# A four-layer graph network on one core: the last experts add into the output by DMA, and the seams between stages are re-ordered

## The chip, the cores and the metric

The kernel runs on one core of a Trainium2 chip, as one program with one launch. The metric is the device time of an execution in microseconds (us). The core's engines run side by side, each in its own order: TensorE (PE in the profile, PEld for its weight loads), VectorE (DVE), ScalarE (ACT), GpSimd (POOL) and SyncE (SP). Sixteen DMA engines move data; ACT, SP and POOL issue the DMAs, each into a queue of its own, and only POOL issues those that take their rows from a list of indices. PSUM, TensorE's result memory, has eight banks.

## The reference

The input is a graph of 1250 nodes with 512 float32 features and 21,250 edges (20,000 and a self-loop each). Four layers follow, and each has the form

```python
xn = _layernorm(x)
x = x + gnn(xn, edges) + mix(xn)
x = x + ffn(_layernorm(x))
```

The parts that differ by layer:

- Layer 0: gnn is GATv2, three times over. Per edge `m = leaky_relu(xl[src] + xr[dst] + ef)`, a softmax over each node's incoming edges of `m @ att`, and the sum of `xl[src]` by these weights; then a layer norm and relu. ffn is a mixture of 8 experts with Sinkhorn routing.
- Layer 1: gnn is two GAT layers with 4 heads, mix an attention without a sequence product (softmax of k over the nodes). ffn has two shared experts and 8 routed ones.
- Layer 2: gnn is an EGC convolution (a normalised sum over neighbours of `x @ W_bases`, combined by weights of `x @ W_comb`), mix a linear attention. ffn has a convolution as router, shared convolutions over the nodes, 10 experts of which each node takes 2, and a layer norm at the end.
- Layer 3: gnn is a GCN, `segment_sum(h[row] * norm, col)`, mix a linear attention. ffn is a mixture of 32 experts, of which each node takes the 2 likeliest; each expert has room for 98 rows (1.25 x 2500 / 32, rounded up):

```python
dest = jnp.where(keep, a * C + pos, N * C)
buf = jnp.zeros((N * C, D)).at[dest].set(x_flat[token], mode='drop').reshape(N, C, D)
o = relu(buf @ W1 + b1) @ W2 + b2
y_flat = segment_sum(o[dest] * w[:, None], token)      # w: the gate, 0 where not kept
y_flat = where(sum of a token's w <= 1e-12, x_flat, y_flat)
```

## The kernel before

**Tiling.** The nodes are 10 tiles of 128 rows (NP = 1280). `x` stays on chip; weights come in through `weight()` (line 138), a DMA of 1 MB on SP's queue into one of four buffers. Most of the code is handed to a planner, which orders each engine's instructions by when it reckons they can run and places the buffers; in a `manual_schedule` block the named engine keeps the order written. `psum(mm, tp, more)` (line 106) divides PSUM's banks for a stage; the next division can be used only when the last reader of the old one is through. `gather` (line 231) and `scatter` (line 239) are POOL's indexed DMAs.

**Stages by time in the trace of before.** 0 to 320: layer 0's attention and the preparation of the edges. To 1590: GATv2, three calls of `gat_layer`. To 1848: `layer0_ffn`. To 2070: `global_attention` (layer 1's mix). To 2830: `gat_dense`. To 3057: `layer1_ffn`. To 3345: `layer2_attn`. To 3728: `layer2_ffn`. To 4125: `layer3_attn`. To 4488: `layer3_ffn`.

**GATv2** (`gat_layer`, line 1200 on). The edges are in 47 groups (FG) of four tiles of 128 (GE); one step of the main loop (line 1460) is one tile. `load(g)` gathers rows of the table xl for a group (four gathers on POOL, 9 buffers). `fields(g)` (line 1255) loads, on SP, the packed node numbers `nb` (4 buffers) and the edge fields into the lower rows of `oh` (3 buffers); `onehot(g)` (line 1272) expands `nb` on ACT. `right(i)` (1282) is TensorE's product of one-hot rows with the tables for xr and the edge term; DVE adds it to xl (1299) and takes the logit (1302); `spread` turns weights into one-hots and the product at line 1353 sums them by node. `finish` ends a block of nodes; `across` (line 1405) turns its rows and queues, tile by tile, the products that make the next layer's tables (`gat_tables`: four products for xl, its write `xl<-tlo` at line 1184, four for xr, its write). The next layer's gathers start when tile 9's xl is written.

**Layer 0's ffn to layer 1.** At the end of `layer0_ffn` (lines 1783 to 1792) each tile gathers its two expert rows, adds them, and is normalised and turned. `global_attention` loads wk at its start and wv later. Beside both, `count` steps build a table of edge counts. `clear` zeroes the expert buffers.

**Layer 2.** `layer1_ffn` and `layer2_attn` share one PSUM division (4, 4, 0), `layer2_ffn` has its own (3, 3, 2). In `layer2_attn` (from line 2590) each tile's neighbour sum `y` takes an mm bank, with attention steps (`go()`) between. In `layer2_ffn` the shared convolutions are a generator of steps (`shared()`), and `experts(..., beside)` runs some of them ahead of the experts and between: `beside(-1)` ten, then two at each point i, none at i = 7 to 9.

**Layer 3's attention.** `tail_steps` (line 2375) finishes layer 2's ffn tile by tile inside layer 3: its `need(t)`, with POOL's order written out, fetches a tile's two expert rows (line 231), adds them, scales and normalises them (`z*ga` on POOL, line 2897), adds them to x (185), and turns the tile. The GCN's product with `L3_gnn_W` follows each tile; the linear attention (`linear_attention_steps`, line 734), whose first weights are loaded at the start, runs beside the GCN's gathers later.

**Layer 3's ffn** (line 3036). The router gives each node's two experts, its places (`putI`) and gates (`w0`). Weights are loaded 11 ahead (line 3051). 20 scatters put rows into `routed_in` (CAP = 98 rows per expert), tiles of x get the b2 term (lines 3149 to 3153, 185) and rows without an expert (1811). Per expert: `xe` in by ACT's queue (3160), four transposes (3164), a copy `xT`, 16 products with w1 (179), relu on ACT (3169), 4 products with w2 (3173), a copy `o` (134), a write to `routed_out`. After all 32, 20 gathers and adds (231, 1811), and ten writes `out<-x` (3188).

## Time and profile before

| what | value |
|---|---|
| median of 3 runs | 4464.39 us (4461.85 to 4471.24) |
| profiled execution, its own time | 4489.82 us |
| its span | 4487.9 us, mean granted clock 0.937 |
| TensorE busy | 3922.2 us, 87% of the span |
| VectorE busy | 2689.5 us, 60% |
| ScalarE busy | 1622.8 us, 36% |
| GpSimd busy | 1351.0 us, 30% |
| DMA | 647.58 MB, mean 144 GB/s |

The profiled execution took 1.9 us more than its span, and 25.4 us more than the median. How to read its rows: a row of the timeline or of the chain gives start, duration, engine, line, operation, output<-input, and in brackets the idle time of that engine before it with what ended it. SPq, ACTq and POOLq are the issues of DMAs. A row of waits gives the waiting engine and line, what it waited for, the total in us, how often, and the longest. A row of a window gives from:to, length, busy time with count for PE, PEld, DVE, ACT, POOL, then TensorE's granted clock, the busy share of the DMA engines and GB/s. By stage, TensorE is busy 1113 of 1270 us in GATv2, 324 of 397 in layer 3's attention, 290 of 363 in its ffn.

### The profile page before, as it was taken

What the parts mean: (1) busy time and instruction counts of PE and PEld (TensorE: products, weight loads), DVE (VectorE), ACT (ScalarE), POOL (GpSimd) and SP (SyncE); (2) the same over time, 40 slices, a digit from 0 to 9 for tenths busy, and PEclk for the clock granted to TensorE, in tenths of its full rate; (3) what the DMA queues carried; (4) which work ended last, traced back from release to release, by engine and by line L of the source; (5) the groups of instructions that cost most, each with busy time, mean ns of one, the idle gap of its engine ahead of it and who ended that gap; (6) DMA issues with size and microseconds to landing.
All of it is one profiled execution on the core that took longest, in us unless ns stands there. A gap on an engine that the chain in (4) does not pass through costs nothing. (4 is left out here: it accounts for less than half of the span.)

```text
span 4487.9 us, 49486 instructions
## 1 busy us (share of the span) xinstructions
PE 3922.2 (87%) x15466; PEld 2415.7 (54%) x15466; DVE 2689.5 (60%) x6338; ACT 1622.8 (36%) x2976; POOL 1351.0 (30%) x1308
## 2 busy tenths in 40 slices
PE   5987998899788867799999999997979896898796
PEld 3434554455354434444788877563546562455474
DVE  5357895888398865523896767314584225687301
ACT  2222442344133375110464446223451232554121
POOL 2017773776466501102000000103131013675102
PEclk9988999999899988899999999999989998997798
DMA  6437664666466423402421110383002653666695
GB/s 220 159 84 211 198 199 150 198 197 193 141 179 189 145 74 108 119 17 64 146 70 42 46 35 29 143 298 128 12 27 83 233 189 119 182 200 199 225 339 181
DMA packets 283001, 647.58 MB, mean 144 GB/s; under 512 B 61673, under 2 KB 108905, under 8 KB 267322
## 3 DMA queue, kind: packets, MB, share of 16 engines
q1 hardware_dynamic: 169290, 357.13, 24.1%
q0 software_dynamic: 73088, 234.75, 18.3%
q10 hardware_dynamic: 40352, 52.44, 3.4%
q8 instruction: 127, 2.08, 0.2%
q14 instruction: 144, 1.18, 0.1%
HBM read 528.87 MB, written 120.65 MB: 145 GB/s over the span
## 5 line engine op out<-in xcount | busy, mean ns | idle before, releaser
L231 POOL DMA_INDIRECT xl<-xl,srcI x564 | 616.8, 1094 | 290.2 <-issue 137.8
L1353 PE MATMUL more<-xl,wT 128*128 128x512 f32 x1128 | 579.7, 601 | 14.5 <-ACT wT L1343 14.0
L1286 PE MATMUL mm<-hl,oh 121*128 121x512 f32 x564 | 419.1, 743 | 73.8 <-DVE s L1299 37.8
L1302 DVE SCALAR_TENSOR_TENSOR junk<-s,att 128x512 f32<-128x512 f32 x534 | 417.9, 783 | 6.8
L1299 DVE TENSOR_TENSOR s<-xl,mm 128x512 f32<-128x512 f32 x534 | 357.8, 679 | 104.0 <-PE mm L1287 48.4
L2129 PE MATMUL more<-hh,e 128*128 128x259 f32 x1600 | 383.7, 385 | 11.7 <-ACT o L2072 8.6
L2129 PEld LDWEIGHTS more<-hh,e 128*128 128x128 f32 x1600 | 295.1, 191 | 75.8 <-issue 17.8
L171 PE MATMUL mm<-w,xnT 128*128 128x512 f32 x640 | 307.8, 620 | 16.6 <-ACT xnT L2388 12.1
L231 POOL DMA_INDIRECT hs<-gcn_h,srcI x188 | 214.6, 1142 | 93.6 <-issue 30.8
L1353 PEld LDWEIGHTS more<-xl,wT 128*128 128x128 f32 x1128 | 196.1, 192 | 74.8 <-issue 27.9
L1287 PE MATMUL mm<-hl,oh 121*128 121x512 f32 x564 | 236.4, 419 | 0.0
L1286 PEld LDWEIGHTS mm<-hl,oh 121*128 121x128 f32 x564 | 111.0, 197 | 215.5 <-issue 117.1
L231 POOL DMA_INDIRECT g<-routed_out,getI x60 | 67.6, 1126 | 488.5 <-DMA routed_out<-o 416.4
L2049 ACT ACTIVATE e<-r,hh 128x512 f32<-128x512 f32 (+1 forms) x240 | 154.2, 646 | 130.7 <-PE more L2129 119.5
L171 PEld LDWEIGHTS mm<-w,xnT 128*128 128x128 f32 x640 | 123.4, 198 | 144.0 <-issue 124.6
L3011 PE MATMUL more<-hl,oh 128*128 128x512 f32 x376 | 161.5, 534 | 30.9 <-DVE oh L2975 10.9
L1273 ACT ACTIVATE oh<-nb 112x512 fp32r<-112x512 bf16 x141 | 88.7, 630 | 273.6 <-DMA nb<-nbt 162.3
L2052 ACT ACTIVATE e<-r,a 128x512 f32<-128x512 f32 (+1 forms) x240 | 152.3, 646 | 71.1 <-DVE e L2054 57.8
L711 PE MATMUL more<-ohs,ohb 128*128 128x512 bf16 x564 | 137.5, 383 | 42.8 <-ACT ohs L695 18.0
L2054 DVE TENSOR_TENSOR e<-e,e 128x512 f32<-128x512 f32 (+1 forms) x240 | 141.5, 596 | 51.2 <-ACT e L2049 44.8
L1287 PEld LDWEIGHTS mm<-hl,oh 121*128 121x128 f32 x564 | 112.4, 199 | 110.1 <-issue 108.4
L1166 PE MATMUL tab<-w,xT 128*128 128x512 f32 x320 | 163.5, 605 | 9.0 <-ACT xT L1415 6.1
(631 smaller groups left out, 7787.8 us busy)
## 6 DMA issues: line engine op xcount, KB each, us to landing
w<-L_ffn_Wp SPq DMA_DIRECT2D x64, 1024.0 KB
w<-L_ffn_table SPq DMA_DIRECT2D x56, 1025.0 KB
neg<-ntab SPq DMA_DIRECT2D x80, 320.0 KB
nb<-nbt SPq DMA_DIRECT2D x141, 128.0 KB
hl<-xr SPq DMA_DIRECT2D x36, 448.0 KB
xr<-tro SPq DMA_DIRECT2D x30, 512.0 KB
xe<-routed_in SPq DMA_DIRECT2D x56, 256.0 KB
routed_out<-o ACTq DMA_DIRECT2D x56, 256.0 KB
```

The costliest lines, as they stand in the source:

```text
L171: self.nc.tensor.matmul(p, lhsT=xT[:, c, t * 128:(t + 1) * 128], rhs=w[:, c, n0:n0 + n], start=c == 0, stop=c == k - 1)
L231: self.nc.gpsimd.indirect_dma_start(out=out, out_offset=None, in_=table, in_offset=bass.IndirectOffsetOnAxis(ap=idx, axis=0), bounds_check ...
L1166: nc.tensor.matmul(d[name], lhsT=xT(c), rhs=L[name][:, c, :], start=c == 0, stop=c == 3)
L1286: nc.tensor.matmul(m, lhsT=s, rhs=hl[:K, 0, :], start=True, stop=False)
L1287: nc.tensor.matmul(m, lhsT=s, rhs=hl[:K, 1, :], start=False, stop=not on_pe(i))
L1299: nc.vector.tensor_tensor(o, d["xl"][:, j, :D], s, op=ALU.add)
L1302: nc.vector.scalar_tensor_tensor(junk, s, 0.0, L["att"], op0=ALU.max, op1=ALU.mult, accum_out=d["lg"][:, j:j + 1])
L1353: nc.tensor.matmul(B[b]["y"], lhsT=d["wT"][:, j, :], rhs=d["xl"][:, j, :D], start=k == 0 and j == 0, stop=last and j == GE - 1)
L2049: nc.scalar.activation(e1[:, :n], R[q, k, 0][:, :n], AF.Exp, bias=HH[q][:, s, 256:257])
L2052: nc.scalar.activation(e2[:, :n], R[q, k, 1][:, :n], AF.Exp, bias=heads[q][0][:, s, 0:1])
L2129: nc.tensor.matmul(ys[j], lhsT=e[:, j * 128:(j + 1) * 128], rhs=HH[q][:, s, :], start=s == 0, stop=s == NT - 1)
L3011: nc.tensor.matmul(y, lhsT=oh, rhs=hl[:, i], start=i + j == 0 and not (self.fast and k), stop=last and i + j == GE)
```

## The change

The change has seven parts. (A) `layer3_ffn` no longer gathers at the end: x with the b2 term is written to `out` ahead of the experts; each row that is scattered carries its node number in column 512 of a new place table `rin3`; a table `gates3` holds each node's first expert and both gates; each expert fetches its rows' gates five experts ahead, scales its output on DVE into `o`, and an indirect DMA adds `o` to `out`. `out` gets 158 more rows for places that nobody took. (B) `gat_layer` puts off the xr products of the last three tiles until the next layer has begun, takes mm banks for the tables at the end, has one more buffer each for nb and oh, and fetches fields three groups ahead; `prepare` begins at step 15. (C) `layer0_ffn` writes out POOL's order for its gathers, and loads wk and wv for layer 1, wv behind a POOL memset. (D) `clear_places` zeroes the new tables in layer 1's mix. (E) `layer2_attn` and `layer2_ffn` share the division (3, 3, 2), and `y` takes a `more` bank. (F) 14 steps ahead of layer 2's experts, and the pause at i = 5 to 7. (G) layer 3's attention weights are loaded behind a POOL memset after tile 0's `need`.

```diff
-    def weight(self, src, k, n):
+    def weight(self, src, k, n, behind=False):
...
         w = self.wp.tile([128, k, n], F32, tag="w", name="w")
+        if behind:
+            self.nc.gpsimd.memset(w[:1, 0, :1], 0.0)
...
     def linear_attention_steps(self, xn, xT, w_qkv, w_out, b_out, qscale, finish, added=None,
-                               need=None):
+                               need=None, ws=None):
...
                 self.tc.tile_pool(name="latmp", bufs=2) as tmp:
-            wk = self.weight(w_qkv[:, D:2 * D], 4, D)
-            wv = self.weight(w_qkv[:, 2 * D:3 * D], 4, D)
+            if ws is None:
+                wk = self.weight(w_qkv[:, D:2 * D], 4, D)
+                wv = self.weight(w_qkv[:, 2 * D:3 * D], 4, D)
+            else:
+                wk, wv, wq = ws
...
                 if half:
-                    wq = self.weight(w_qkv[:, 0:D], 4, D)
+                    if ws is None:
+                        wq = self.weight(w_qkv[:, 0:D], 4, D)
...
         step = [0]
+        rest = []
+        ending = [False]
...
         def fields(g):
-            nb = p.tile([128, GE * 128], BF16, tag="nb", name="nb", bufs=4)
+            nb = p.tile([128, GE * 128], BF16, tag="nb", name="nb", bufs=5)
             nc.sync.dma_start(nb, self.nbt[g])
-            s = p.tile([128, GE * 128], F32R, tag="oh", name="oh", bufs=3)
+            s = p.tile([128, GE * 128], F32R, tag="oh", name="oh", bufs=4)
...
                 for t in whole:
-                    for f in self.gat_tables(nxt, p, t, lambda c, t=t: X[t][:, c, :],
-                                             lambda: self.bank("tab", [128, D])):
+                    fs = self.gat_tables(nxt, p, t, lambda c, t=t: X[t][:, c, :],
+                                         lambda: self.mm() if ending[0] else
+                                         self.bank("tab", [128, D]))
+                    if t >= NT - 3:
+                        rest.extend(fs[5:])
+                        fs = fs[:5]
+                    for f in fs:
...
         fields(1)
+        fields(2)
         onehot(0)
+        for f in L.pop("rest", ()):
+            f()
...
                     onehot(g + 1)
-            if j == 2 and g + 2 < FG:
-                fields(g + 2)
-            if i >= 6 and i % 3 == 0:
+            if j == 2 and g + 3 < FG:
+                fields(g + 3)
+            if i >= 15 and i % 3 == 0:
...
         bias_cur(NB - 1)
+        ending[0] = True
...
                     late.popleft()[1]()
+        if nxt is not None:
+            nxt["rest"] = rest
...
             self.layer0_ffn_to_layer1_attn()
-            with self.weights(), self.psum():
-                self.layer1_ffn()
+            banks = ExitStack()
+            with self.weights():
+                with self.psum():
+                    self.layer1_ffn()
+                banks.enter_context(self.psum(3, 3, 2))
                 self.layer2_attn()
-            with self.psum(3, 3, 2):
-                self.layer2_ffn()
+            self.layer2_ffn()
+            banks.close()
...
                     self.counting = self.count_blocks(range(CB), True) if fast else iter(())
-                    self.layer0_ffn(xn, xnT)
+                    ws = self.layer0_ffn(xn, xnT)
...
                         steps = self.count_steps()
-                    self.global_attention(xn, xnT, steps)
+                    self.global_attention(xn, xnT, ws, steps)
...
                     done += 1
-            for t in range(NT):
-                for j in range(2):
-                    g = tmp.tile([128, D], F32, tag="g", name="g", bufs=6)
-                    self.gather(g, obuf[:, :], getI[:, t, j:j + 1])
-                    self.add_scaled(t, g, G[:, t, j:j + 1])
-                self.ready(t)
-                self.norm_tile(t, xn[:, t, :])
-                self.transpose_tile(xnT[:, :, t * 128:(t + 1) * 128], xn[:, t, :])
-                self.count(1)
+            wk = self.weight(I["L1_mix_WkT"], 4, D)
+            with self.tc.manual_schedule(engines={mybir.EngineType.Pool}):
+                for t in range(NT):
+                    for j in range(2):
+                        g = tmp.tile([128, D], F32, tag="g", name="g", bufs=6)
+                        self.gather(g, obuf[:, :], getI[:, t, j:j + 1])
+                        self.add_scaled(t, g, G[:, t, j:j + 1])
+                    self.ready(t)
+                    self.norm_tile(t, xn[:, t, :])
+                    self.transpose_tile(xnT[:, :, t * 128:(t + 1) * 128], xn[:, t, :])
+                    self.count(1)
+                wv = self.weight(I["L1_mix_WvT"], 4, D, behind=True)
             g1.close()
+        return wk, wv
...
+    def clear_places(self, p):
+        nc = self.nc
+        self.rin3 = self.dram.tile([32 * CAP, D + 2], F32, name="routed_in3")
+        self.gtab = self.dram.tile([NP + 128, 4], F32, name="gates3")
+        zero = p.tile([128, D + 2], F32, name="zero3")
+        nc.gpsimd.memset(zero, 0.0)
+        nc.sync.dma_start(self.gtab[NP:, :], zero[:, :4])
+        nc.sync.dma_start(self.out[NP:, :], zero[:, :D])
+        nc.gpsimd.iota(zero[:, D:D + 1].bitcast(I32), pattern=[[0, 1]], base=NP,
+                       channel_multiplier=1)
+        for e in range(32):
+            nc.sync.dma_start(self.rin3[e * CAP:(e + 1) * CAP, :], zero[:CAP])
...
-    def global_attention(self, xn, xnT, steps):
+    def global_attention(self, xn, xnT, ws, steps):
...
-            wk = self.weight(I["L1_mix_WkT"], 4, D)
+            wk, wv = ws
+            self.clear_places(p1)
...
-            wv = self.weight(I["L1_mix_WvT"], 4, D)
...
-    def tail_steps(self, xn, xnT):
+    def tail_steps(self, xn, xnT, behind=None):
...
                             f(u + n - i)
+                if t == 0 and behind is not None:
+                    behind()
...
                     go()
-                    y = self.mm([128, parts * 256])
+                    y = self.more([128, parts * 256])
...
-                    for _ in range(10 if i < 0 else 0 if 7 <= i < 10 else 2):
+                    for _ in range(14 if i < 0 else 0 if 5 <= i < 8 else 2):
...
             xn = p.tile([128, NT, D], F32, name="xn")
-            need = self.tail_steps(xn, xnT)
+            ws = []
+            def load():
+                ws.extend(self.weight(I["L3_mix_w_qkvT"][:, i:i + D], 4, D, behind=True)
+                          for i in (D, 2 * D, 0))
+            need = self.tail_steps(xn, xnT, load)
...
                     lambda o, d: nc.vector.tensor_scalar(o, d, 1e-8, None, op0=ALU.add),
-                    added)
+                    added, ws=ws)
...
             ahead = 11
-            xn = p.tile([128, NT, D], F32, name="xn")
+            xn = p.tile([128, NT, D + 2], F32, name="xn")
+            nc.gpsimd.memset(xn[:, :, D:], 0.0)
+            nc.gpsimd.iota(xn[:, :, D].bitcast(I32), pattern=[[128, NT]], base=0,
+                           channel_multiplier=1)
...
             for t in range(NT):
-                self.norm_tile(t, xn[:, t, :])
+                self.norm_tile(t, xn[:, t, :D])
...
             putI = p.tile([128, NT, 2], I32, name="putI")
-            getI = p.tile([128, NT, 2], I32, name="getI")
+            gate = p.tile([128, NT, 4], F32, name="gate")
...
                     for j in range(2):
-                        self.scatter(self.rin, putI[:r, t, j:j + 1], xn[:r, t, :], "moe")
+                        self.scatter(self.rin3, putI[:r, t, j:j + 1], xn[:r, t, :], "moe")
+                nc.vector.tensor_tensor(
+                    prod, ohs[0], self.iota[:, :NE].unsqueeze(1).to_broadcast([128, NT, NE]),
+                    op=ALU.mult)
+                nc.vector.memset(gate, 0.0)
+                nc.vector.tensor_reduce(gate[:, :, 0], prod, AX.X, ALU.add)
...
                     nc.vector.tensor_tensor(w0[:, :, j], w0[:, :, j], s, op=ALU.mult)
-                nc.vector.tensor_scalar(dest, dest, float(ROWS - 1), None, op0=ALU.min)
-                nc.vector.tensor_copy(getI, dest)
...
                                         op=ALU.mult)
+                nc.vector.tensor_copy(gate[:, :, 1:3], w0)
+                nc.sync.dma_start(self.gtab[:NP, :].rearrange("(t p) c -> p t c", p=128), gate)
...
                 self.add_to_x(t, y)
-                self.add_scaled(t, xn[:, t, :], none[:, t:t + 1])
+                self.add_scaled(t, xn[:, t, :D], none[:, t:t + 1])
+                r = rows(t)
+                nc.scalar.dma_start(self.out[t * 128:t * 128 + r, :], self.x[:r, t, :])
+            tok = p.tile([CAP, NE], I32, name="tok")
+            for i in range(0, NE, 8):
+                nc.scalar.dma_start(
+                    tok[:, i:i + 8].bitcast(F32),
+                    self.rin3[i * CAP:(i + 8) * CAP, D].rearrange("(e c) -> c e", c=CAP))
+            gates = {}
+            def fetch(e):
+                gates[e] = tmp.tile([CAP, 4], F32, tag="g", name="g", bufs=8)
+                self.gather(gates[e], self.gtab[:, :], tok[:, e:e + 1])
+            for e in range(5):
+                fetch(e)
...
                 er = slice(e * CAP, (e + 1) * CAP)
-                xe = tmp.tile([CAP, D], F32, tag="xe", name="xe", bufs=3)
-                nc.scalar.dma_start(xe, self.rin[er, :])
+                xe = tmp.tile([CAP, D], F32, tag="xe", name="xe", bufs=4)
+                nc.scalar.dma_start(xe, self.rin3[er, :D])
+                if e + 5 < NE:
+                    fetch(e + 5)
+                g = gates.pop(e)
+                d = tmp.tile([CAP, 2], F32, tag="d", name="d", bufs=4)
+                nc.vector.tensor_scalar(d[:, :1], g[:, :1], float(e), None, op0=ALU.is_equal)
+                nc.vector.tensor_tensor(d[:, 1:], g[:, 1:2], g[:, 2:3], op=ALU.subtract)
+                nc.vector.scalar_tensor_tensor(d[:, 1:], d[:, :1], d[:, 1:], g[:, 2:3],
+                                               op0=ALU.mult, op1=ALU.add)
...
                                      start=f == 0, stop=f == 3)
-                o = tmp.tile([CAP, D], F32, tag="o", name="o")
-                self.evac(o, y)
-                nc.scalar.dma_start(self.rout[er, :], o)
+                o = tmp.tile([CAP, D], F32, tag="o", name="o", bufs=3)
+                nc.vector.tensor_scalar(o, y, d[:, 1:], None, op0=ALU.mult)
+                nc.gpsimd.indirect_dma_start(
+                    out=self.out, out_offset=bass.IndirectOffsetOnAxis(ap=tok[:, e:e + 1],
+                                                                         axis=0),
+                    in_=o, in_offset=None, bounds_check=NP + 127, oob_is_err=True,
+                    compute_op=ALU.add)
...
                         ahead += 1
-            for t in range(NT):
-                for j in range(2):
-                    g = tmp.tile([128, D], F32, tag="g", name="g", bufs=4)
-                    self.gather(g, self.rout[:, :], getI[:, t, j:j + 1])
-                    self.add_scaled(t, g, w0[:, t, j:j + 1])
-                r = rows(t)
-                nc.sync.dma_start(self.out[t * 128:t * 128 + r, :], self.x[:r, t, :])
...
          for k, v in arrays.items()}
-    out = nc.dram_tensor("out", (N, D), F32, kind="ExternalOutput").ap()
+    out = nc.dram_tensor("out", (NP + 128, D), F32, kind="ExternalOutput").ap()
...
     r = run_bass_kernel_spmd(nc, [arrays], core_ids=[0])
-    return r.results[0]["out"]
+    return r.results[0]["out"][:N]
```

## The prediction

> **What bounds the kernel now.** I began with the page's busy shares, to see whether any engine is full.
>
> ```profile
> PE 3922.2 (87%) x15466; PEld 2415.7 (54%) x15466; DVE 2689.5 (60%) x6338; ACT 1622.8 (36%) x2976; POOL 1351.0 (30%) x1308
> ```
>
> TensorE is busy for 87% of a span of 4487.9 us. The other 566 us are the seams between stages, and every edit works on a seam. Second came the chain that ended last, at the end of the run.
>
> ```profile
> 4439.99 3.45 PE mm L3173 x8
> 4443.46 0.59 ACT o L134
> 4444.07 2.95 DMA routed_out<-o
> ...
> 4476.85 5.24 DMA g<-routed_out,getI
> 4482.19 0.75 DVE x L1811
> ```
>
> Expert 31's last product ends at 4443.44. Then TensorE stands idle to 4487.9: 44.4 us in which 20 rows-gathers and their adds run. Third, slices of the expert loop (engines PE, PEld, DVE, ACT, POOL; granted clock, DMA share, GB/s).
>
> ```profile
> 4268.00:4280.00 12.00, 12.00 (x70) 8.33 (x70) 0.57 (x1) 3.25 (x9) 0.00 (x0) 1.00 0.99 354
> 4412.00:4424.00 12.00, 12.00 (x74) 8.39 (x73) 1.04 (x2) 2.89 (x7) 0.00 (x0) 1.00 0.11 35
> ```
>
> In the loop TensorE alone is full (22.21 us per three experts on the chain, 7.40 each); POOL does nothing, and DMA is nearly full until the weights run out at about 4408. Fourth, the timeline and waits at the other seams, shown with each part.
>
> **A, the adding DMAs.** *End.* The 44.4 us become: o on DVE 0.75 (priced as L1811), a POOL issue 1.05, one adding DMA. No add is in the trace. Below, it costs what the indexed write routed_in<-xn takes, 2.64 us from issue to landing; above, that plus the gather's 5.24 (old row read, then written), 7.88. I take the middle, 5.2. Then 7.0 us are left: **-37.4** (-40 to -34).
>
> *Pace.* All adds write one tensor, so each waits for the one before. POOL's period is 1.05 + 0.3 of wait + 5.2 = 6.5 us (4.0 to 9.2 by the bounds) under the 7.40 of an expert; the gate gather (1.05) is issued during the landing. [...] The row: 20 gathers today leave POOL every 1.3 us, overlapping. [...] At the gathers' 1.3 us the adds would hide altogether[...]. [...] It costs nothing up to 7.40, and 32 us for each us above.
>
> *Bytes.* An expert moves 2.097 MB of weights, 0.2 in, 0.2 out; with the read of the old rows 2.7 MB. At 340 GB/s, my mean of the slices in 4220 to 4400 (318 to 354), that takes 7.94 us, 0.54 too long, for 26 experts 14 us. The last weight load was issued at 4403.8 and used at about 4440, so some 30 us of lead cover it: 0. Without that cover it is +14.
>
> *Start.* Expert 0 waits for the 20 scatters (last landing 4200.64), then xe (2.50). Moved in ahead of xe on ACT's queue: ten writes of x to out, of which only the last can be late, and four loads of tok, each of 98 x 8 single words. On POOL come five gate gathers; on SP the gate table's write, behind weight loads already issued. Two rows differ on such loads:
>
> ```profile
> 256.39 0.39 SPq L601 DMA_DIRECT2D s<-stab  x1
> 276.59 7.07 SPq L2926 DMA_DIRECT2D dinvb<-dinv  x1
> ```
>
> The first moves 1280 short pieces onto 128 partitions, and DVE uses them at 259.44, 3.05 us later. The second stands 7.07 us behind a load of 1177 words onto 107 partitions, while the DMA share in 278 to 284 is 0.10. [...] By the second row four loads hold xe up for 4 x 784/1177 x 7.07 = 18.8 us; by the first for four issues, 1.6 us, and some engine time. I take the first: **+6**, being 1.6 for tok, 0.9 for the last out write and 3.5 for DVE's small operations (0.15 each), which wait for tok (3), a gather (1.05 + 2.6) and may stand ahead of expert 0's xT copy. Range +2 to +19. The new DVE work behind the scatters lies under their 24 us on POOL.
>
> **B, GATv2's seams.**
>
> ```profile
> 752.31 0.33 SPq L1184 DMA_DIRECT2D xl<-tlo  x1
> 758.60 1.03 POOL L231 DMA_INDIRECT xl<-xl,srcI  x1 [12.22 <-DMA xl<-tlo]
> 770.00:780.00 10.00, 6.97 (x23) 4.20 (x21) 5.70 (x15) 0.00 (x0) 7.99 (x9) 0.83 0.68 196
> SPq L1259 <- PE mm L1287: 30.5, 6, 14.8
> ACT oh L1273 <- DMA nb<-nbt: 18.0, 2, 11.9
> ```
>
> The next layer's first gather needs the table xl written up to tile 9. From 706 to 741 TensorE is full, and among its work are wr(7) and wr(8), eight passes of 0.43 us each, ahead of the last mix; nobody reads wr before that layer has begun. Deferring two removes 2 x 3.44 = 6.9 us at each of two seams (wr(9) was behind): **-13.8** (-14 to -7). The 10.3 us put off fall where TensorE stands for 9.66 us before 765.7 or in the ramp behind, where POOL sets the pace. Without that cover they return whole.
>
> The ramp: the gathers give a group per 5.6 us, DVE needs 8.3, yet DVE is busy 5.70 of 10 at 770. The two waits (third layer's start, 1180 to 1250; second's, 756 to 812) tell why: SP's in-order queue waits for an oh buffer with nb's load behind it, and ACT's one-hot waits for nb. A fourth oh, a fifth nb and one group more of lead should free about half of it. DVE lost some 21 us between 760 and 810; I count 5 of each of two ramps: **-10** (-24 to 0).
>
> **C, layers 0 and 1; G, layer 3.** In both, weights were loaded next to the write that the first gather waits for.
>
> ```profile
> 3729.03 0.33 ACTq L2367 DMA_DIRECT2D routed_out<-o  x1
> 3736.03 1.05 POOL L231 DMA_INDIRECT g<-routed_out,getI  x1 [54.80 <-DVE oh L2975]
> ```
>
> This write takes 7.0 us to its gather, under 4 MB of weights issued from 3723.70. Unloaded, before layer 2's attention, it takes 2.8 (3057.28 to 3060.08). G puts 3 of the 4 MB behind a POOL instruction after tile 0's needs (about 3757); k's products use them from about 3820, 60 us later: **-4** (-6 to +4, the last if SP's queue holds up layer 3's own loads behind them). In C the same wait is 5.8 us (1810.05 to 1815.83), but only one of the loads moves, and iota (1.2) leaves POOL's row of gathers: **-3** (-5 to 0).
>
> **D, clearing the place table.** 34 writes on SP, 14.6 us at 0.43 an issue and 6.4 MB, lie in layer 1's mix, where DMA share is 0.06 to 0.5. The count's loads of ohb are queued behind them on SP, and TensorE waits for those: **+2** (0 to +8).
>
> **E, one PSUM division for layer 2.**
>
> ```profile
> 3347.70 6.69 PE L2731 MATMUL tp<-ident,z 128*128 128x128 f32 x36 [10.68 <-DVE x L185]
> ```
>
> TensorE waits 10.68 us for attention's last read of the old division, though z was there at about 3340. DVE is next: it is busy 11.44 of 14 us in 3332 to 3346 and full from 3360. So only 3 of the 7 come free; three mm banks in place of four may cost the attention's first 15 steps 1. **-2** (-7 to +5). The exchange itself moves to where TensorE idles 17.55 us for gathers.
>
> **F, 14 convolution steps.**
>
> ```profile
> 3488.27 1.09 PE L160 MATMUL tp<-ident,xe 128*128 128x128 f32 x4 [9.94 <-DMA xe<-routed_in]
> ```
>
> Four more steps are 32 passes of 0.265 us, 8.5 us, in a hole of 9.94; the convolution then ends that much sooner: **-8** (-8.5 to -3, less if the pause at 5 to 7 leaves TensorE waiting there).
>
> **The sum.** -37.4 + 6 - 13.8 - 10 - 3 - 4 + 2 - 2 - 8 = **-70.2 us**. It is made against the profiled execution: span 4487.9 and 1.9 around it, 4489.8, which becomes 4419.6. That execution lies 25.4 us above the median of the runs, 4464.4; the same difference there gives **4394**. The half-widths 3, 7, 4, 12, 3, 5, 4, 6, 3, added in squares, make 18: 4374 to 4412 for this case.
>
> **Rivals.**
> (1) *The seams hand their gain on.* B's ramp is held by POOL's gathers and the Wl and Wr loads (DMA share 0.68 at 770) instead of buffers, B's seams give half, C, E and G nothing: -37.4 + 6 - 6.9 + 2 - 6 = -42.3, 4422. For it: in both ramps POOL is busy 8 of 10. Against: the 30.5 us that SP's queue waits.
> (2) *The adds pace the experts somewhat*: at 8.4 us, +32: 4426. For it: the DMA share of 0.92 to 0.99 in which they land.
> (3) **Slower**: the same mechanism at full size. Without the adds' pace the sum is -70.2; it is used up where the period reaches 7.40 + 70.2/32 = 9.6 us, and the kernel is slower by 0.2% from 9.9. At 10.5 it is -70.2 + 99.2 = +29, 4493. For it: a landing of 9.2 us needs only the upper bound of 7.88 and the full DMA queues. Against: the gather's 5.24 was itself measured with other gathers queued.
> (4) *Nothing changes at F and B*: the planner that orders TensorE's work may place moved steps where they were: 22 us less gain, 4416, close to rival 1 and counted there.
>
> **How the numbers follow.** The likeliest 0.62; seams 0.20; adds at 8.4, 0.06; slower 0.07; a larger gain, below 4366, 0.05. The range from 4364 to 4448 leaves out the last two and tails of the others, some 0.18. About 0.2% (8.9 us) is what a measurement of this kernel can tell from no change. Between seams and slower lies a little for the same: faster 0.89, same 0.03, slower 0.08.
>
> **What would show it.** A: TensorE's last product within 10 us of the end; adds on POOL under 7.4 us apart, and experts still 7.40; the first transposes of xe about 4203 + 6 on this clock. B: 7 us less from the last mix to the first gather, DVE at 8 of 10 and more in the ramps. C, G: 3 us from write to gather. E: the 10.68 near 7. F: the 9.94 near 1. The prediction is wrong if adds are more than 7.4 us apart, tok takes over 10 us, or the deferred products stand ahead of work that DVE needs.

## The result, and the profile after

The changed kernel takes **4435.69 us** (median of 4 runs, 4431.85 to 4439.00), beside 4464.78 us (4461.85 to 4471.24) for the kernel before on the same chip. The ratio is 0.9938 with a 95% interval of 0.9925 to 0.9951, so 29.1 us are gained where the forecast had 70.2. The sign was right, the size was not.

First the page's head and busy shares of the kernel after.

```profile
span 4437.2 us, 49701 instructions
...
PE 3910.3 (88%) x15466; PEld 2410.0 (54%) x15466; DVE 2699.0 (61%) x6432; ACT 1611.9 (36%) x2960; POOL 1408.8 (32%) x1360
```

TensorE does as much as before (3922.2); the gain lies in what stands between its work. Next the chain that ended last, kernel after (start, duration, what).

```profile
4371.91 9.48 DMA out<-o,tok
...
4381.48 0.76 DVE o L3259
...
4400.03 3.45 PE mm L3256 x8
...
4404.93 4.47 DMA out<-o,tok
...
4410.22 4.43 DMA out<-o,tok
...
4415.46 4.48 DMA out<-o,tok
...
4420.76 4.48 DMA out<-o,tok
...
4427.47 1.51 POOL out L3260
```

Before, the chain ended in a product, a write and a row of gathers. Now it ends in a row of adds, each after the one before, up to the last, which starts as soon as its own `o` is there. The same DMA lands 9.48 us after its start at 4371.91 and 4.43 at 4410.22: between the two the stream of weights ran out (the DMA engines' share is 0.80 in 4370 to 4390 and 0.34 in 4390 to 4410). Over all 32 the trace gives 4.4 to 11.9 us. The last product ends at 4426.4 (4422.78 + 3.60), 10.8 us from the end, where it was 44.5.

Windows of the expert loop, kernel after (from:to, length, busy of PE, PEld, DVE, ACT, POOL, then granted clock, DMA share, GB/s).

```profile
4210.00:4230.00 20.00, 19.92 (x113) 13.32 (x112) 4.33 (x14) 3.95 (x11) 5.70 (x5) 1.00 1.00 343
...
4330.00:4350.00 20.00, 13.32 (x74) 9.98 (x75) 2.76 (x9) 2.75 (x8) 5.19 (x4) 0.87 0.69 219
...
4390.00:4410.00 20.00, 19.96 (x122) 14.23 (x121) 2.57 (x7) 4.60 (x13) 4.54 (x4) 1.00 0.34 53
```

TensorE is full at first. By 4330 it is busy two thirds of the time and its clock is granted at 0.87. Near the end the DMA engines are a third busy and it is full again. The waits of TensorE from 4140 on, kernel after (who and line, for what: total us, times, longest):

```profile
PE mm L181 <- DVE o L3259: 16.4, 7, 5.6
...
PE mm L181 <- DVE xT L136: 4.9, 1, 4.9
...
PE tp L3247 <- DMA xe<-routed_in: 3.7, 1, 3.7
```

The largest is the wait for `o`: it has three buffers, each held until its add has landed (DVE's `o` waits 69.5 us for adds, eight times, 11.2 at the longest), and so PSUM's banks and the next products are held too, for those 16.4 us.

**Where the time went, by landmarks.** Each stretch runs from one event to the next. The second column is a second profile of the kernel before (span 4464.4; before_again below), and "second profile" is that of after_again; I compare with before_again, because the profile that the forecast was worked from was 23.5 us longer, 19.0 of them by the end of GATv2 and 9.3 between layer 3's first gather of `gcn_h` and its places.

| stretch, ending at | before | after | after, second profile | forecast |
|---|---|---|---|---|
| last weighted sum of GATv2 (B) | 1564.5 | 1550.7: -13.8 | 1550.3: -14.2 | -23.8 |
| first gather of `l0moe_out` (C) | 231.0 | 227.7: -3.3 | 227.4: -3.6 | -3 |
| first `xe` of layer 2's experts (D, E) | 1675.9 | 1671.3: -4.6 | 1676.2: +0.3 | 0 |
| first gather of layer 3 (F, G) | 250.2 | 243.5: -6.7 | 242.5: -7.7 | -12 |
| places cast to `putI` (untouched but for G's loads) | 428.1 | 422.8: -5.4 | 425.6: -2.5 | 0 |
| end of the span (A) | 314.7 | 321.3: +6.6 | 309.2: -5.5 | -31.4 |
| sum | 4464.4 | 4437.2: -27.2 | 4431.2: -33.2 | -70.2 |

Between the two profiles of the kernel after, a stretch moves by up to 5 us, and by 12 in A's row, so a single entry is good to some 5 us at best. The table still places the miss: 26 to 38 us of it are A, some 9 are B, some 5 are F and G.

### The profile page after: what moved, and what is told of

It reads as the page before. It is cut to its first block, busy times and chain, and to the rows that moved or that the text cites. A ratio compares the mean times of both kernels' runs of the same rounds, so it can differ in the third digit from the quotient of the medians.

```text
span 4437.2 us, 49701 instructions
## 1 busy us (share of the span) xinstructions
PE 3910.3 (88%) x15466; PEld 2410.0 (54%) x15466; DVE 2699.0 (61%) x6432; ACT 1611.9 (36%) x2960; POOL 1408.8 (32%) x1360
## 3 DMA queue, kind: packets, MB, share of 16 engines
q0 software_dynamic: 76608, 236.00, 19.0%
## 5 line engine op out<-in xcount | busy, mean ns | idle before, releaser
L1294 PE MATMUL mm<-hl,oh 121*128 121x512 f32 x564 | 419.2, 743 | 31.9 <-DVE s L1307 14.1
L2170 PE MATMUL more<-hh,e 128*128 128x259 f32 x1600 | 380.3, 383 | 11.2 <-ACT o L2113 8.0
L1281 ACT ACTIVATE oh<-nb 112x512 fp32r<-112x512 bf16 x141 | 88.8, 630 | 262.0 <-DMA nb<-nbt 204.2
L2033 PE MATMUL mm<-w,xnT 128*128 128x258 f32 x640 | 159.0, 392 | 4.2 <-DVE junk L2017 3.6
L1351 ACT COPY wT<-tp 128x512 f32<-128x512 f32 x141 | 81.9, 583 | 221.0 <-PE tp L1348 219.1
```

What stands on the lines that cost most here:

```text
L1294: nc.tensor.matmul(m, lhsT=s, rhs=hl[:K, 0, :], start=True, stop=False)
L2033: nc.tensor.matmul(m, lhsT=chunk(layer, c)[:, t * 128:(t + 1) * 128], rhs=w[:, c, :], start=c == 0, stop=c == k - 1)
L2170: nc.tensor.matmul(ys[j], lhsT=e[:, j * 128:(j + 1) * 128], rhs=HH[q][:, s, :], start=s == 0, stop=s == NT - 1)
```

## The experiments

Two theories stood against each other for A. **Contention**: an add lands late because the weights fill the DMA queues, and 32 adds in a row, each waiting for the last, then set the pace. **Start**: the pace is harmless and A loses at its start, on the new loads, gathers and small DVE operations ahead of expert 0. A third was that the gain of the other parts is what fell short. The kernels that ran on one chip share its runs of the kernel before; the four chips' own times for it were 4460, 4472 (twice) and 4499 us, so ratios are compared, not times.

### before_again: the kernel before, profiled a second time

> The kernel before, unchanged, profiled a second time: its first profiled execution took 4489.8 us, 25 more than the median of its runs, so stage lengths of that trace may be too long. If the 25 us lie in stages that the change touches, this trace (about 4465) shows GATv2 shorter by 10 to 13 and layer 3's attention shorter by about 10 than the first, so that of the 32.7 and 11 us that the two traces seemed to gain there only some 20 and 1 remain. Rival: the extra is spread over all stages in proportion (0.6 % each), and GATv2 then comes out 7 shorter, layer 3's attention 2.

It took 4466.28 us in the profiled execution. This is the column "before" above. GATv2 is 19.0 us shorter than in the first profile, more than was expected; the stretch in layer 3's attention is 9.3 shorter, as expected. In the profile that the forecast used, the start of the third layer (last weighted sum of the second to the first of the third) took 15.6 us longer than here.

### undo_A: the experts gather at the end again

```diff
-                o = tmp.tile([CAP, D], F32, tag="o", name="o", bufs=3)
-                nc.vector.tensor_scalar(o, y, d[:, 1:], None, op0=ALU.mult)
-                nc.gpsimd.indirect_dma_start(
...
-                    compute_op=ALU.add)
+                o = tmp.tile([CAP, D], F32, tag="o", name="o")
+                self.evac(o, y)
+                nc.scalar.dma_start(self.rout[er, :], o)
...
+            for t in range(NT):
+                for j in range(2):
+                    g = tmp.tile([128, D], F32, tag="g", name="g", bufs=4)
+                    self.gather(g, self.rout[:, :], getI[:, t, j:j + 1])
+                    self.add_scaled(t, g, w0[:, t, j:j + 1])
+                r = rows(t)
+                nc.sync.dma_start(self.out[t * 128:t * 128 + r, :], self.x[:r, t, :])
```

The place and gate tables and their clearing (D) go too.

> The changed kernel with the old end: experts written to routed_out and gathered, no adding DMAs, no place table (parts A and D undone, B, C, E, F, G kept). Theory (the adds cost in the loop what they save at the end): by the traces, from the last scatter to the end took 288.9 us before and 293.7 after, so A is worth +4.8 and this kernel takes about 4431 (4424 to 4438). Rival (A brought its forecast -31 and the seams brought nothing): about 4467, the time of before.

4445.51 us, ratio 0.9963 (0.9951 to 0.9975), between the two expectations. From the places to the end it takes 313.4 us, as the kernel before (314.7, and 315.8 in the first profile) and inside the spread of the kernel after (309.2 to 321.3). So by the trace A gives nothing, though by the whole time this kernel is 0.25% behind. The trace has that difference before the places: `putI` is cast at 4129.8 here, at 4116.0 and 4122.0 in the kernel after. Of what was undone, only D's clearing works in those stages; the next run separates it.

### undo_A_keep_D: the same, with D's clearing kept

> The old end, but with the place table and gate table still laid out and cleared in layer 1's mix (part A undone, part D kept although nothing reads it). Theory 1 (the layout of the buffers in memory, or the order of layer 1's mix, that came with D is what makes undo_A slower ahead of the experts): this kernel loses undo_A's extra and comes to about 4430, 0.9935 of before. Theory 2 (undo_A's stages ahead of the experts were slow by chance): like undo_A when that is measured often, between 0.993 and 0.996.

4440.60 us, 0.9931 (0.9910 to 0.9951), beside 0.9929 (0.9909 to 0.9950) for the kernel after on the same chip: with and without A the time is the same. Places to end: 315.0. So A as a whole is worth 0 within about 13 us by the clock, and -6 to +7 by the traces. Why undo_A's own ratio is worse than this one's stays open. The two intervals just touch. D is no cause that the traces support: with it `putI` is cast at 4131.6 here and at 4130.4 in plain_write below, as late as in undo_A. Another placement of buffers, or chance, was not separated.

### no_stream: the weights of the experts are not loaded after the first eleven loads

The experts from the sixth on reuse earlier weights.

```diff
             def load(i):
+                if i >= 11:
+                    ws.append(ws[i - 10])
+                    return
```

> The changed kernel without the stream of weights in the expert loop: the first eleven weights are loaded and experts from the sixth on use them again, which leaves out 53 MB of loads and makes the output another. Theory (an add is slow because its rows queue behind weights on the DMA engines): adds land in about 4.5 us throughout as they do now at the end, they come every 7.4 us with the experts, TensorE has no stalls: about 4405 (4398 to 4412). Rival (an add takes 9 us by itself, by its read and write of the same rows, whatever else runs): adds stay 9 us apart for the first 23 experts, 4436.

4417.53 us, 0.9903 (0.9886 to 0.9919). Places to end: 296.1, so 18.6 less than before. POOL's timeline of this kernel (start, duration, line, and in brackets the idle time before and what ended it), and a window as above:

```profile
4272.59 1.52 POOL L3263 DMA_INDIRECT out<-o,tok  x1 [5.07 <-DVE d L3244]
...
4279.56 1.52 POOL L3263 DMA_INDIRECT out<-o,tok  x1 [4.08 <-DVE o L3262]
...
4287.53 1.52 POOL L3263 DMA_INDIRECT out<-o,tok  x1 [5.07 <-DVE d L3244]
```

```profile
4230.00:4260.00 30.00, 29.92 (x179) 21.09 (x179) 5.51 (x18) 6.47 (x18) 10.49 (x9) 1.00 0.30 55
```

The adds now come 6.97 and 7.96 us apart by turns, 7.5 on average (4174.73 to 4407.09 for 31), which is the experts' own pace. Each lands 4.2 to 4.6 us after its start, all through the loop. What ends POOL's wait is DVE, not the add before. TensorE is full. With the stream away, at a DMA share of 0.30 where the kernel after has 0.99 (4230 to 4250), the adds do what the forecast said, so the weights are what makes them late. Where they meet, in the DMA engines or at the memory, no run separates.

The time is still 5 us above the expected range. First transposes to last product take 248.6 us where the kernel before takes 240.2, with no wait for `o` at all. Some 5 of these 8.4 us lie before expert 0's last product. The other 3.3 are spread: TensorE needs 7.50 us per expert with no stall (7.39 before), and takes the transposes of two experts at a time where it took three. They are the same in o_deep and plain_write, so they belong to the changed loop and not to late adds; no run takes them apart.

### plain_write: the rows are written, not added

Each expert's rows overwrite `out`; the sum is left out.

```diff
-                    in_=o, in_offset=None, bounds_check=NP + 127, oob_is_err=True,
-                    compute_op=ALU.add)
+                    in_=o, in_offset=None, bounds_check=NP + 127, oob_is_err=True)
```

> The changed kernel in which each expert's rows are written over out's rows in place of being added (same rows, same order, same wait for the one before; the sum over a node's two experts and x is left out). Theory (under the stream of weights an add's time is mostly the queueing of its rows behind weights, and reading the old rows is the smaller part): the writes are 6 to 8 us apart while weights stream (9.25 and 8.65 with adds), 4 after, and part of the 30 us comes back: 0.989 to 0.992 of before. Rival (the read and add of old rows is what takes the time): writes at the experts' own pace of 7.5 us, no stall, like the kernel without the stream, about 0.988 or less.

4430.58 us, 0.9901 (0.9881 to 0.9920); places to end 298.6. POOL's timeline:

```profile
4276.81 1.01 POOL L3260 DMA_INDIRECT out<-o,tok  x1 [5.54 <-DMA out<-o,tok]
...
4286.02 1.00 POOL L3260 DMA_INDIRECT out<-o,tok  x1 [6.84 <-DMA out<-o,tok]
...
4292.60 1.01 POOL L3260 DMA_INDIRECT out<-o,tok  x1 [4.21 <-DMA out<-o,tok]
```

Writes still wait for one another, at a period of 7.90 us in the stream (4184.09 to 4381.56 for 25) and about 4 after it. So adding in place of writing is some 1.3 us of a period of 9.25, 0.5 of it POOL's issue (1.52 where the write has 1.01); most of the period stays with the plain indexed write among the weights. The write alone lands 3.0 us after its start out of the stream and 5.7 to 8.6 in it. As 7.90 is near the experts' pace, it does little harm.

### o_deep: ten buffers for `o` instead of three

```diff
-                o = tmp.tile([CAP, D], F32, tag="o", name="o", bufs=3)
+                o = tmp.tile([CAP, D], F32, tag="o", name="o", bufs=10)
```

> The changed kernel with ten buffers instead of three for o, an expert's scaled output that waits for its add. Theory (the chain of adds is the slower one, about 9.25 us each while weights stream, and TensorE stands because o has no free buffer): TensorE's stalls of some 30 us go, the weights end sooner, and the adds left over then drain at 5.25 us each; the last add is still late, so only about half is won: about 4422 (4412 to 4430), adds still about 9 us apart while weights stream. Rival (TensorE stands because weights or gates come late): no change, 4436.

4440.41 us, 0.9951 (0.9937 to 0.9966): no gain. The expectation failed here, and this is the most useful of the misses. A window in the loop and one at the end, then POOL's wait:

```profile
4230.00:4260.00 30.00, 29.92 (x180) 21.09 (x178) 5.62 (x20) 6.46 (x18) 7.80 (x6) 1.00 0.98 332
...
4410.00:4440.00 30.00, 0.00 (x0) 0.00 (x0) 0.00 (x0) 0.00 (x0) 6.04 (x4) 0.52 0.26 35
```

```profile
POOL out L3260 <- DMA out<-o,tok: 118.4, 20, 8.3
```

TensorE is full, has no wait for `o`, and ends at 4408.8, 31 us ahead of the end. But now POOL waits 118.4 us for its own adds (67.9 in the kernel after): while the stream lasts they come 9.45 us apart (4177.26 to 4375.68 for 21), and the end of the kernel is where the 32nd lands. The waits for `o` were a symptom. The chain of adds is the limit, with or without room ahead of it.

### after_again and after_third: the kernel after, on two more chips

> The changed kernel itself, unaltered, beside the others on one chip, to put a firm number on what undo_A is compared with. In undo_A's trace the stretch from the last place computation to the end was 313.4 us against 321.3 in the changed kernel, yet its runs were slower (0.9963 of before against 0.9938). If both figures hold, this kernel is again at 0.994 of before, about 10 us under undo_A; if undo_A's distance was chance, this kernel comes out at 0.996 to 0.998.

> The changed kernel once more, beside hybrid22_act on one chip: 0.993 of before (0.991 to 0.995).

4439.62 us, 0.9929 (0.9909 to 0.9950), and 4481.05 us, 0.9957 (0.9944 to 0.9970), the second just above its expected range. All three ratios are alike within their intervals. What differs is the adds' period in the stream: 9.25, 8.68 and 9.03 us. The wait for `o` follows it; in the profile of after_again it is

```profile
PE mm L181 <- DVE o L3259: 7.1, 6, 2.4
```

instead of 16.4, and from the places to the end 309.2 us instead of 321.3.

### undo_B: GATv2 as before

```diff
-                    if t >= NT - 3:
-                        rest.extend(fs[5:])
-                        fs = fs[:5]
...
-            if j == 2 and g + 3 < FG:
-                fields(g + 3)
-            if i >= 15 and i % 3 == 0:
+            if j == 2 and g + 2 < FG:
+                fields(g + 2)
+            if i >= 6 and i % 3 == 0:
```

The buffers of nb and oh and the bank for the tables go back too.

> The changed kernel with GATv2's layers as they were (part B undone: no deferred products, the old buffers and the old lead). By the second trace of before, GATv2 ends 13.7 us later there than in the changed kernel: about 4449 (4444 to 4454), +13.7. By the forecast of the parts, +23.8: 4460. By the first trace of before, +32.7: 4468.

4460.13 us, 0.9974 (0.9965 to 0.9982), against 0.9929 on the same chip. B is worth 20 us by the clock, with some 10 either way, which fits the forecast's 23.8 as well as the traces' 14. By the trace it is 14.1 (GATv2's last sum at 1564.4 against 1550.3); both profiled executions are the fastest of their kernel's runs. It is the largest part of the gain. Cut finer, the 14 us are not where the forecast put them:

| place | before_again, undo_B | with B | forecast |
|---|---|---|---|
| layer 0's first 12 groups | 90.6, 90.3 | 83.1 to 83.5: -7 | 0 |
| group 40 to the last product, first and second layer | 48.2, 48.1; 49.1, 48.0 | 42.5 to 43.7; 42.4 to 43.5: -5 each | -6.9 each |
| last product to the next layer's first, both seams | 63.7, 61.9; 59.0, 58.6 | 60.6, 62.0; 60.0, 58.9: about 0 | 0 |
| second layer's first 12 groups | 87.3, 86.0 | 88.8, 92.3: +4 | -5 |
| third layer's first 12 groups | 87.0, 87.0 | 86.8 to 87.0: 0 | -5 |

The third row is not steady either: in all three profiles on after_third's chip, where only kernels with the change were profiled, the two stretches are 72 to 76 us. Why is open.

TensorE's timeline at the end of the first layer, kernel before (`more<-xl,wT` are the weighted sums, `tab<-w,xT` the tables' products), then the kernel after, where those products write `mm`:

```profile
737.65 1.88 PE L1166 MATMUL tab<-w,xT 128*128 128x512 f32 x4
...
739.37 1.88 PE L1353 MATMUL more<-xl,wT 128*128 128x512 f32 x4
```

```profile
723.93 4.46 PE L1361 MATMUL more<-xl,wT 128*128 128x512 f32 x10
...
733.86 15.48 PE L1172 MATMUL mm<-w,xT 128*128 128x512 f32 x32 [0.69 <-ACT xT L1423]
```

The last sums now run through in one row; tile 9's xl and the three put-off xr stand in one block behind them.

A window of the first ramp in undo_B, then in after_again:

```profile
410.00:430.00 20.00, 17.16 (x61) 9.93 (x60) 18.01 (x41) 4.19 (x7) 15.33 (x16) 0.91 0.70 198
```

```profile
410.00:430.00 20.00, 18.64 (x72) 11.02 (x71) 19.97 (x53) 6.47 (x10) 16.69 (x17) 1.00 0.76 213
```

DVE, the busiest engine in both (18.01 and 19.97 of 20 us), does 53 instructions in place of 41.

### prep_early: the preparation starts at step 6 again, a single execution

```diff
-            if i >= 15 and i % 3 == 0:
+            if i >= 6 and i % 3 == 0:
```

> The changed kernel with GATv2's prepare() begun at step 6 again in place of 15 (the rest of B kept), for one look at layer 0's ramp: from its first weighted sum to that of group 12 it takes 90.3 to 90.6 us in both traces of before and in undo_B, 83.1 to 84.8 in the changed kernel and its variants. If the fourth oh buffer, the fifth nb buffer and the longer lead gave these 7 us, it stays near 83.5; if the later preparation did (its loads, and what POOL computes of them, stand in SP's queue among the groups' loads), it goes back to about 90.

4485.32 us in the profiled execution, beside 4498.85 for the kernel before and 4485.09 for the profile of the kernel after on that chip. The first layer's first 12 groups take 90.1 us, as before the change. So the 7 us of that row come from the later preparation, not from buffers. The whole time doesn't show them; one execution can't, at this spread.

### undo_F: ten steps ahead of layer 2's experts again

```diff
-                    for _ in range(14 if i < 0 else 0 if 5 <= i < 8 else 2):
+                    for _ in range(10 if i < 0 else 0 if 7 <= i < 10 else 2):
```

> The changed kernel with 10 convolution steps ahead of the experts and the pause at 7 to 9, as before (part F undone). In the changed kernel's trace TensorE still waits 9.89 us ahead of expert 0, with the same 79 convolution passes ahead of it: by that the four more steps did not get into the hole and this kernel is the same within 2 us. By the forecast it is 8 us slower.

4448.59 us, 0.9948 (0.9930 to 0.9966), which can't be told from 0.9929 to 0.9957. From the first `xe` to layer 3's first gather it takes 246.4 us. On the same chip plain_write and hybrid22, which have the change, take 245.5 and 245.3; on other chips kernels with it take 241.2 to 246.7. So F is worth about 1 us here and at most some 5, of 8. TensorE's timeline of the kernel after shows why:

```profile
3449.72 1.09 PE L162 MATMUL tp<-ident,xe 128*128 128x128 f32 x4 [9.89 <-DMA xe<-routed_in]
...
3450.60 2.29 PE L2736 MATMUL more<-form,cw 128*128 128x312 f32 x4
```

The hole is still 9.89 us (it was 9.94), and the steps that were to fill it come after the transposes of the first expert. The planner, which fixes TensorE's order from its own reckoning, put them there.

### hybrid24, hybrid22, hybrid22_act: adds for the last experts alone

If the chain of adds is what costs, a short chain should keep the tail's gain and lose the cost. The experts below S write `routed_out` as before; their gathers run during the last ones; only those from S on add.

```diff
+                if e < S:
+                    self.evac(o, y)
+                    nc.scalar.dma_start(self.rout[er, :], o)
+                else:
+                    nc.vector.tensor_scalar(o, y, d[:, 1:], None, op0=ALU.mult)
+                    nc.gpsimd.indirect_dma_start(
...
+                if e == S - 1:
+                    for t in range(NT):
+                        for j in range(2):
+                            gr = xn[:, (2 * t + j) % NT, :D]
+                            self.gather(gr, self.rout[:S * CAP, :], getI[:, t, j:j + 1])
+                            self.add_scaled(t, gr, wl[:, t, j:j + 1])
+                        r = rows(t)
+                        nc.sync.dma_start(self.out[t * 128:t * 128 + r, :], self.x[:r, t, :])
```

With S = 24 and the writes of x on ACT's queue:

> The changed kernel with the old way for experts 0 to 23 (written out, and all 20 gathers while experts 24 to 27 run, when POOL has nothing to do) and adding DMAs for experts 24 to 31 alone, with six buffers for o. Theory (an add costs 9.1 to 9.3 us while weights stream and 5.2 after, and the chain of adds is what ends last): the gathers take 26 us and end, with the write of x, about 33 us after expert 23; eight adds of 5.2 us then end some 15 to 20 us after TensorE; TensorE is not held up; from the last place computation to the end about 290 us in place of 321: about 4405 (4398 to 4415). Rival (the adds cost little and something else in the loop holds TensorE up): 4436 or more.

With S = 22, the writes on SP's queue and nine buffers for `o`:

> The hybrid again, since its first form held TensorE up in another way (x's writes, placed on ACT, stood ahead of relus and TensorE waited 28 us): now experts 0 to 21 in the old way, x's writes on SP's queue, the 20 gathers into the ten slots of the router's input, nine buffers for o, adding DMAs for experts 22 to 31. Theory (chain of adds: 5.2 each once the weights are through, gathers and x's write some 36 us after expert 21, no stall of TensorE): the last add lands about 21 us after TensorE's last product, and the stretch from the last place computation to the end is about 296 us against 309 to 321: 0.990 of before, 10 to 25 us under the changed kernel. Rival (something else in the loop holds TensorE up): no gain on the changed kernel.

With the last ten `o` and `xT` on ACT and their scales worked out early:

> The hybrid of experts 22 to 31 by adding DMAs, with what held TensorE up for 16 us in hybrid22 taken away: there o, on DVE, stood behind the adds to x that wait for gathers. Here the last ten experts' o and xT are on ACT and their ten scales are worked out before the gathers begin. Theory (only the chain of adds and this queueing on DVE stand between A and its gain): no stall of TensorE, last add about 21 us after its last product, the stretch from the last place computation to the end near 299 us against 309 to 321: 0.989 to 0.991 of before. Rival (the hybrid moves the wait once more): 0.993 to 0.995, like the changed kernel.

4447.64 us, 0.9944 (0.9925 to 0.9964); 4443.58, 0.9938 (0.9923 to 0.9952); 4478.32, 0.9954 (0.9941 to 0.9968). All three missed what was expected of the short chain, and none beats the kernel after. Each found another wait. In hybrid24, ACT's relus stood behind a write of x that waited for the gathers' adds:

```profile
4354.22 0.81 ACT L3256 ACTIVATE hT<-mm,b 128x98 f32<-128x98 f32 x3 [13.97 <-DVE x L1852]
```

In hybrid22, `o` stands behind those same adds in DVE's order (at 4343.46, 4358.36 and 4370.39, where the adds had waited up to 26.40, 4.13 and 3.12 us for their gathers), and TensorE's waits show it late:

```profile
PE mm L181 <- DVE o L3267: 16.1, 2, 8.9
```

In hybrid22_act, a window near the end has the DMA engines full and TensorE at a third:

```profile
4380.00:4400.00 20.00, 6.69 (x26) 3.12 (x25) 10.88 (x15) 1.87 (x5) 14.20 (x13) 0.60 0.98 342
```

POOL's gathers and SP's writes of x fall into that window. TensorE's waits there end on nothing that the profile names (8.6 us), on a relu (3.7) and on `o` (1.1), and none on a weight; so the cause of this stall stays open.

Their stretches from the places to the end, 318.6, 314.8 and 313.6 us, are about that of the kernel before. In the first two the wait is plain: what the old ending does behind TensorE's last product stands, in the loop, ahead of work on ACT and DVE that TensorE needs.

## Why the prediction failed in size, step by step

**A, pace: the step that failed.** The forecast put an add's landing at 5.2 us, the middle of 2.64 and 7.88, and so the period at 6.5, under the experts' 7.40, at no cost. After the stream the trace gives less than that: a start to landing of 4.4 to 4.5 us with POOL's issue (1.51) inside it, and a period of 5.3. Under the stream the period is 8.7 to 9.25, of which some 0.8 is not landing: about 8 to 8.5 us, single ones from 4.4 to 11.9. POOL's timeline of the kernel after, three rows from the stream and two from after it:

```profile
4207.60 1.52 POOL L3260 DMA_INDIRECT out<-o,tok  x1 [9.64 <-DVE d L3242]
4209.43 1.07 POOL L233 DMA_INDIRECT g<-gates,tok  x1 [0.30 <-issue]
4216.78 1.53 POOL L3260 DMA_INDIRECT out<-o,tok  x1 [6.29 <-DMA out<-o,tok]
...
4410.22 1.51 POOL L3260 DMA_INDIRECT out<-o,tok  x1 [3.78 <-DMA out<-o,tok]
...
4415.46 1.51 POOL L3260 DMA_INDIRECT out<-o,tok  x1 [3.74 <-DMA out<-o,tok]
```

The middle was taken between two rows measured with the DMA engines less than full: their share is 0.27 in the 5 us around the write's row and 0.72 in the 6 us around the gather's, against 0.98 and 1.00 in the windows of the stream above. The forecast had the slice with a share of 0.99 among its views and used it for bytes only, not for the latency of a transfer under it. The upper bound of 7.88 was no bound.

That the adds go one after another, and not every 1.3 us like the gathers of before, held. Every row above that ends in `<-DMA out<-o,tok` is such a wait (14 of them, 67.9 us, for POOL in the kernel after), though no run here shows what an add without it would do. In o_deep these waits, 118.4 us, alone set the end. Pricing the adds as a chain was right, and the price was wrong.

Counted along the adds of the first profile, 23 periods of 9.254 us are 23 x 1.854 = 42.6 us over the experts' pace, and the last 8, at 5.66, win back 8 x 1.74 = 13.9. So the pace costs 28.7 us where the forecast had 0. In the second it is 24 x 1.285 - 7 x 2.10 = 16.1; in the third 23 x 1.633 - 8 x 1.26 = 27.5. The last seven or eight adds run beside few other transfers and catch up; the forecast's third rival, which multiplied its excess by 32, left that out.

**A by stretches.** TensorE's first transposes, expert 0's last product and the last product of all cut the row of A into four. The entries are differences to the mean of the two profiles of before (31.1, 11.0, 229.1 and 44.1 us), so each column adds up by construction.

| stretch | forecast | after | after_again | after_third | no_stream | o_deep |
|---|---|---|---|---|---|---|
| places to first transposes | +6 | +5.6 | +6.0 | +6.0 | +5.5 | +5.4 |
| to expert 0's last product | in the 6 | +4.6 | +4.6 | +3.9 | +5.2 | +4.9 |
| to expert 31's last product | 0 | +29.1 | +13.9 | +23.8 | +3.3 | +3.6 |
| to the end of the span | -37.4 | -33.3 | -30.5 | -29.1 | -33.2 | -13.0 |
| sum | -31.4 | +6.0 | -6.1 | +4.5 | -19.2 | +0.9 |

The third row is the pace as TensorE feels it, 3.3 of it without late adds. Ten buffers for `o` clear it and move the loss to the last row, where the adds drain; taking away the stream clears both.

**A, start.** The first transposes come 5.4 to 6.0 us later. The forecast's sign for them was 6, though its sum had only 2.5 for what stands ahead of them. The dear reading of tok's four loads, 4.7 us each, is out: POOL's first gather, which waits for the first of them, starts 2.96 us after its issue.

```profile
4145.15 0.36 ACTq L3219 DMA_DIRECT2D tok<-routed_in  x1
...
4148.11 1.08 POOL L233 DMA_INDIRECT g<-gates,tok  x1 [4.65 <-DMA tok<-routed_in]
```

These 2.96 us are near the 3.05 of the cheap row, which the forecast took as its estimate. The DVE term, 3.5 of the forecast's 6, came on top. Timeline of expert 0, kernel before, then after:

```profile
4203.18 1.57 PE L3164 MATMUL tp<-ident,xe 98*128 98x98 f32 x8 [4.97 <-DMA xe<-routed_in]
...
4204.76 6.15 PE L179 MATMUL mm<-xT,w 128*128 128x98 f32 x32
```

```profile
4152.65 0.91 PE L3247 MATMUL tp<-ident,xe 98*128 98x98 f32 x4 [3.69 <-DMA xe<-routed_in]
...
4157.41 0.15 DVE L3240 TENSOR_SCALAR d<-g 98x1 f32<-98x1 f32 x1 [3.69 <-DMA g<-gates,tok]
...
4157.80 0.56 DVE L136 COPY xT<-tp 128x392 f32<-128x392 f32 x1
...
4158.42 6.40 PE L181 MATMUL mm<-xT,w 128*128 128x98 f32 x32 [4.85 <-DVE xT L136]
```

The transposes were done at 4153.6, but `xT` is copied only at 4157.80: in DVE's order it stands behind a `d` that waits for its gate, and that `d` is the fourth expert's. From the transposes to the first product it takes 5.8 us in place of 1.6. So the start is about +10, not +6.

**A, bytes.** 0, as forecast: no wait for weights is among TensorE's in the loop of the kernel after. That an add moves the old rows as well was an estimate, and the profile doesn't show it: POOL's queue moves 236.00 MB where it moved 234.75, which is about `o` once for each expert (6.42 MB) in place of the gathers (5.24).

**A, end.** From 44.1 to 10.8, 13.6 and 15.0 us: -33 to -29 (forecast -37.4). The forecast's 7.0 us were `o`, an issue and a landing. In the first profile nothing was queued: the last add starts 1.1 us after the last product and lands 4.4 later, but then 5.4 us more pass to the end of the span, which had no term. In the other two the last add starts 3.7 and 5.1 us after the product, so 2.6 and 4.0 of their end are queue.

So A's miss of 37.4, 25.3 and 35.9 us divides into 29.1, 13.9 and 23.8 in the loop, about 4 at the start, and 4 to 8 at the end.

**B.** -14 in the trace for a forecast of -23.8. The seams' mechanism was right: the products for xr left the way of the last mixes, -5 at each where -6.9 was said. Its own sign looked at the wrong stretch: from the last mix to the first gather it takes no less than before (17 to 21 us, from 17 to 18). The ramps were wrong. The forecast gave them -10 from waits for buffers, read in part from the one layer start that was 15.6 us long in that execution; in the third layer they gained nothing, and the second lost 4. That the put-off products cost this, a case that the forecast listed among those that would refute it, is not shown: in the kernel after they ran until 749.3, while the first gathered rows came at 752.7, and prep_early, which has them too, takes 85.8 us for those groups. The 7 us in the first layer, from the preparation's later start, had no term at all. So a good part of the -14 is luck.

**C and G** were right: -3.3 for -3, and the wait that C was to shorten, from the last write of layer 0's experts to their first gather, is 3.7 us in all three profiles where it was 6.2 and 8.4. G's write to gather, in the kernel before, second profile, then the kernel after:

```profile
3714.43 0.33 ACTq L2367 DMA_DIRECT2D routed_out<-o  x1
...
3721.53 1.05 POOL L231 DMA_INDIRECT g<-routed_out,getI  x1 [55.55 <-DVE oh L2975]
```

```profile
3690.38 0.33 ACTq L2408 DMA_DIRECT2D routed_out<-o  x1
...
3693.18 1.12 POOL L233 DMA_INDIRECT g<-routed_out,getI  x1 [62.15 <-DVE oh L3024]
```

7.1 us became 2.8, the same as the unloaded wait before layer 2's attention on which the forecast built its 4.2.

**D** cost nothing that undo_A_keep_D or the landmarks show (forecast +2), though 2 us are within their scatter.

**E.** Its row did as forecast and better:

```profile
3303.50 0.90 PE L2774 MATMUL tp<-ident,z 128*128 128x128 f32 x4 [5.12 <-DVE z L224]
```

10.68 became 5.12 (3.57 in the second profile). But from these transposes to the first `xe` of the experts it takes 146.2 us in place of 140.3, so 5.9 are given back in that stage (146.1 in undo_F, so F's steps are not why). With D, the stretch holds -4.6 to +0.3. No run undoes E alone; by these rows it is at most a gain of the order of the forecast's 2.

**F** went as the fourth rival said: the planner left the hole at 9.89. From 1 to 5 us remain of 8.

**The rivals.** The second, adds that pace the experts, is what came true, at 8.7 to 9.25 instead of 8.4, with the fourth for F. The forecast gave the second 6 in 100. Of the first, the ramps that gain nothing from buffers came true in the second and third layers; its doubt of C and G did not.

## What to carry to other kernels

A transfer's latency is to be taken from a row with the same load on the DMA engines: the rows of the forecast, at shares of 0.27 and 0.72, gave no upper bound for adds at 0.98 and 1.00, and this chain of one transfer at a time would have needed a margin of twice (4.4 to some 8 us), not of a tenth. Ten buffers in front of the chain did not cure it (o_deep, 0.9951). A shorter latency did (no_stream, 296.1 us from the places to the end in place of 309.2 to 321.3); fewer links, tried three ways, moved the wait elsewhere (0.9938 to 0.9954), in two of them to work of ACT and DVE that stood behind the gathers' adds (13.97 and 16.1 us); independent targets for the adds were not tried. And when a ramp or a stall is to be priced, two executions of the same kernel should show it first.

## What the runs showed of the hardware

- One and the same adding DMA (98 rows of 512 float32) took 4.2 to 4.6 us from its start to its landing with the DMA engines a third busy (no_stream, share 0.30) and 4.4 to 11.9 beside the stream of weights (kernel after, share 0.69 to 1.01 in windows of 20 us from 4170 to 4390); the indexed write without the add had a period of 7.90 in the stream and 3.8 to 4.3 in the three behind it (plain_write).
- An adding DMA kept POOL for 1.51 to 1.56 us (kernel after), the same one without the add for 0.97 to 1.01 (plain_write), a gather of gates for 1.03 to 1.08 (kernel after).
- A load of 98 x 8 single words had landed by 2.96 us after its issue (kernel after, 4145.15 to 4148.11). With four of them and everything else that was put ahead of `xe`, the first transposes came 5.4 to 6.0 us later.
- In 4330 to 4350 of the kernel after, TensorE was busy 13.32 of 20 us and its granted clock was 0.87; with the stalls gone it was 1.00 in the windows of 4230 to 4260 in o_deep and no_stream, at 29.92 of 30.
- The two profiled executions of the kernel before differ by 19.0 us by the end of GATv2 alone.
